# A decoder layer in one kernel: the softmax shifts of a cross-attention set through one transpose, an addition on VectorE, and another order of the first loads

## The chip, the cores and the metric

The kernel runs on one core of a Trainium2 chip. A core has five engines with a queue of instructions each: TensorE (PE in the profile; its loads of weights are listed apart as PEld), VectorE (DVE), ScalarE (ACT), GpSimd (POOL) and SyncE (SP), which here issues most of the DMAs. Each engine runs its own queue in order; semaphores make one engine wait for another. TensorE writes its results into eight banks of PSUM, from which VectorE and ScalarE read them; everything else lies in SBUF, in 128 partitions.

The metric is the device time of one execution in microseconds. It is given as the median of several runs; a profile is taken from one execution more, which has a time of its own.

## The reference

One layer of a decoder for x of 4 x 512 x 512 numbers in float32: three blocks, each behind a layer norm and added to x.

```python
x = x + _L0_attn_ref(_layernorm(x), wq_comp, wq_up, wk, wv, ..., out_w1, out_w2)   # 16 heads, window of 128
x = x + _L0_xattn_ref(_layernorm(x), ctx, ctx, mask, Wq, Wk, Wv, Wo)                # cross attention
x = x + _L0_ffn_ref(_layernorm(x), w_gate, w_up, w_down)                            # ternary feed-forward
```

The change touches the second block above all. It has 4 batches, 512 queries, 1024 keys, and 16 query heads of 32 columns in 4 groups that share keys and values:

```python
Q = (query @ Wq).reshape(b, q_len, G, Hpg, dh) / math.sqrt(dh)
K = (key @ Wk).reshape(b, kv_len, G, dh)
V = (value @ Wv).reshape(b, kv_len, G, dh)
scores = jnp.einsum('bqghd,bkgd->bghqk', Q, K) + m * rel
scores = jnp.where(mask[:, None, None, None, :], scores, neg)
out = jnp.einsum('bghqk,bkgd->bqghd', jax.nn.softmax(scores, axis=-1), V)
```

The layer norm is `(x - mean) / sqrt(var + 1e-5)` over the 512 columns of a row.

## The kernel before

The program is one long list of steps; the order of TensorE's work, and in places of ScalarE's and VectorE's, is that of the code (`manual_schedule`), while the queues of the other engines are ordered by a scheduler. The stages follow one another: a prologue (0 to 60 us of the profile), 64 units of local attention (60 to 640), a transition, cross attention (712 to 1345), its end, and the feed-forward block (from about 1400).

**The prologue.** SyncE loads, in the order of the code, the first 128 rows of x (L67), then through `fold_load` (L504) the first block of out_w1 (L509, 0.25 MB), x's rows 1 to 3 of 128 (L518), the second block of out_w1, the first of out_w2 (L512, 1 MB), and then wq_comp, wk, wv, the cosines and sines and the two norm weights (L522 to L533). The norm weights are multiplied on VectorE into kw_col (L535). On TensorE two chains are interleaved by `fill` (L908 to L912): `before(0)` takes the statistics of x's rows, normalises them (h, L125), transposes them (tr_ps, L133) and makes qc_ps (L620); `fold` multiplies out_w1 by out_w2 into one weight (w1T through L133 and L134, then f_ps, L678), one step of it for each count of `fill`.

**A layer norm's scale.** `norm_of` (L100) is used for the queries of cross attention and the rows of the feed-forward block, 12 times in all: VectorE's statistics (L87, L88), an addition of epsilon on GpSimd (L106, tiles veps2 and rstd2 with one buffer each), a power of -0.5 on GpSimd (L80), then ScalarE's shift (L113, L116) and the normalised rows (L120, called from `norm_rows`).

**Cross attention.** It works in 16 sets, m = 0 to 15, each of one batch and one of the four heads of every group. A set has 512 queries in 4 tiles of 128 (qt), 4 groups (g) and two halves of the keys (h). The softmax needs the maximum of each query's row. Two sets ahead, `row_max` (L1040) computes scores without the maximum for 128 queries and 512 keys at a time (s_ps, L1045), and VectorE reduces each to one column of nms (L1049, negated). `merge` (L1074) takes the minimum over the two halves. `shift` (L1084) turns the result from columns into rows, splits each number into a rounded part (a copy in F32R) and the rest, and moves both as two more rows, R_TOP and R_TOP + 1, into the operand qss of the scores, whose multiplication then subtracts the maximum. It takes these steps: transposes into nm_ps (L1088, a PSUM bank), a copy to nmT (L1092), a scaling by `parts` (L1093), a multiply and add from nm_ps (L1096), and the moves on SyncE (L1100, which the profile lists under the helper's line L187).

The main loop runs over steps of one tile of 128 keys, 8 for each set. In each step TensorE has: three row-max products for the set that lies ahead, two multiplications of the scores (st, L1107), a fourth row-max product between them, two more scores, what is planned beside it (`extra`: shift, queries, keys, values, outputs), the second half of the scores (L1118), and the weighted values (o_ps, L1143) of the step before. ScalarE takes two exponentials of 128 x 1024 for each step (L1125); GpSimd adds them to the sums of the softmax (L1132, 2.38 us each), and later multiplies by the reciprocal. `merge(m)` comes at the end of step 8m - 3, `shift(m)` is planned at step 8m - 2, and the scores of set m begin at step 8m.

The tiles nm_ps, s_ps, and other short products share the three PSUM banks of the pool `smp` (tag "sm"); st has two buffers of two banks, o_ps one bank.

From step 87 on, `side_rows` normalises and quantises pairs of rows of 128 for the feed-forward block, beside the attention: eight pieces each, for pairs beginning at steps 87, 93, 102, 108, 114 and 120.

Of the kernel before, what the change touches and what calls it, by code (L numbers as in the profile page):

```python
# [12 lines left out]
F32 = mybir.dt.float32  # L13
F32R = mybir.dt.float32r
# [4 lines left out]
ALU = mybir.AluOpType  # L19
AX = mybir.AxisListType  # L20
PSUM = bass.MemoryType.PSUM

P = 128
B, T, D = 4, 512, 512
# [3 lines left out]
G = 4  # L28
# [22 lines left out]
def decoder_layer(  # L51
# [48 lines left out]
    def norm_of(t0, n):  # L100

        mv = row_stats(t0, n)
        veps, rstd, shift = (
            small.tile([P, QT], F32, name=name, bufs=1) for name in ("veps2", "rstd2", "shift")
        )
        nc.gpsimd.tensor_tensor(veps[:, :n], mv[:, :n, 1], least[:, 0, :n], ALU.add)  # L106
        power_neg_half(rstd[:, :n], veps[:, :n])
        return mv, rstd, shift, n

# [75 lines left out]
    def move(out, in_, by=None):  # L185

        (by or nc.sync).dma_start(out=out.bitcast(F32), in_=in_.bitcast(F32))  # L187
# [305 lines left out]
    with tc.tile_pool(name="aw", bufs=1) as aw, tc.tile_pool(name="akv", bufs=2) as akv, \  # L493
# [10 lines left out]
        def fold_load(n, second=True):  # L504

            g, h = divmod(n, HG)
            if n not in w1s:
                w1s[n] = ap.tile([P, D], F32, name="w1")
                nc.sync.dma_start(out=w1s[n], in_=out_w1[g, ts(h, P)])  # L509
            if h == 0 and second:  # L510
                w2s[g] = ap.tile([P, DC, D], F32, name="w2")
                nc.sync.dma_start(  # L512
                    out=w2s[g], in_=out_w2[g * D:(g + 1) * D].rearrange("(c p) o -> p c o", p=P)
                )

        fold_load(0, False)
        for t in range(1, QT):
            nc.sync.dma_start(out=xres[:, t, :], in_=x[0, ts(t, P)])  # L518
        for n in (1, 0):
            fold_load(n)  # L520
        wqc_sb = aw.tile([P, DC, P], F32, name="wqc_sb")
        nc.sync.dma_start(out=wqc_sb, in_=wq_comp.rearrange("(c p) n -> p c n", p=P))  # L522
        wkv_sb = aw.tile([P, DC, 2 * P], F32, name="wkv_sb")
# [381 lines left out]
        with tc.manual_schedule(  # L905
            engines={mybir.EngineType.PE, mybir.EngineType.Activation, mybir.EngineType.DVE}
        ):
            for i, _ in enumerate(before(0)):  # L908
                if i in (0, QT - 1):
                    fill(5 if i else 1)  # L910
                elif i >= QT:
                    fill(6 if i == 9 else 2)  # L912
        with tc.manual_schedule(engines={mybir.EngineType.PE, mybir.EngineType.Activation}):
# [98 lines left out]
    with tc.tile_pool(name="b1", bufs=1) as b1, \  # L1012
# [27 lines left out]
        def row_max(m, i):  # L1040

            b, hh = divmod(m, HG)
            hf, g, qt = i // 16, i // 4 % 4, i % 4
            s_ps = smp.tile([P, T], F32, tag="sm", name="s_ps")
            nc.tensor.matmul(  # L1045
                s_ps, lhsT=qss[hh][0:R_TOP, g, ts(qt, P)], rhs=kss[b % 2][0:R_TOP, g, ts(hf, T)],
                start=True, stop=True,
            )
            nc.vector.tensor_reduce(nms[m][:, qt, g, hf:hf + 1], s_ps, AX.X, ALU.max, negate=True)  # L1049

        def row_maxima(m, i):

            b, hh = divmod(m, HG)
            hf, g, qt = i // 8, i // 4 % 2 * 2, i % 4
            s_ps = stp.tile([P, 2, T], F32, name="st")
            for j in range(2):
                nc.tensor.matmul(
                    s_ps[:, j, :], lhsT=qss[hh][0:R_TOP, g + j, ts(qt, P)],
                    rhs=kss[b % 2][0:R_TOP, g + j, ts(hf, T)], start=True, stop=True,
                )  # L1060
            nc.vector.tensor_reduce(
                nms[m][:, qt, g:g + 2, hf], s_ps, AX.X, ALU.max, negate=True
            )

        parts = small.tile([2 * G, 2], F32, name="parts", bufs=1)
        nc.vector.tensor_reduce(
            parts[:, 0:1], ident[:2 * G, 0:2 * G].rearrange("p (g h) -> p g h", h=2)[:, :, 1],
            AX.X, ALU.add,  # L1070
        )
        nc.vector.tensor_scalar(parts[:, 1:2], parts[:, 0:1], -2.0, 1.0, ALU.mult, ALU.add)

        def merge(m):  # L1074

            full = small.tile([P, QT, G, 2], F32, tag="nm3", name="nm3", bufs=2)
            both = nms[m].rearrange("p q g h -> p (q g) h").unsqueeze(2)
            nc.vector.tensor_reduce(
                full.rearrange("p q g h -> p (q g) h"), both.to_broadcast([P, QT * G, 2, 2]),
                AX.X, ALU.min,  # L1080
            )
            nms[m] = full

        def shift(m):  # L1084

            ps = smp.tile([2 * G, T], F32, tag="sm", name="nm_ps")
            for qt in range(QT):
                nc.tensor.transpose(  # L1088
                    ps[:, ts(qt, P)], nms[m][:, qt].rearrange("p g h -> p (g h)"), ident
                )  # L1090
            nmT = bx.tile([2 * G, T], F32R, tag="t", name="nmT", bufs=3)
            nc.scalar.copy(nmT, ps)  # L1092
            nc.scalar.activation(  # L1093
                nmT.bitcast(F32), nmT.bitcast(F32), AF.Copy, scale=parts[:, 1:2]
            )
            nc.vector.scalar_tensor_tensor(  # L1096
                nmT, ps, parts[:, 0:1], nmT.bitcast(F32), ALU.mult, ALU.add
            )
            for g in range(G):
                move(qss[m % HG][R_TOP:R_TOP + 2, g, :], nmT[2 * g:2 * g + 2, :])  # L1100

        def scores(m, kt, i):
            b, hh = divmod(m, HG)
# [123 lines left out]

        def side_queries(m, half):
            if half == 0:
                nms[m] = small.tile([P, QT, G, 2], F32, tag="nm2", name="nm2", bufs=2)  # L1230
            queries(m, half)
            if half == 1:
                send_queries(m)
# [45 lines left out]


        with tc.manual_schedule(engines={mybir.EngineType.PE}):
            nms[0] = small.tile([P, QT, G, 2], F32, tag="nm2", name="nm2", bufs=2)
            first.values(0)
            first.turn(2, nc.scalar)
            first.keys(2)
            first.values(1)
            first.turn(3)
            first.keys(3)
            first.send(1)
            for i in range(G * QT):  # L1290
                row_maxima(0, i)
                if i in (2, 4):
                    side_queries(1, i // 4)
                if i in (6, 8):
                    first.values(i // 2 - 1)
                if i == 8:
                    batches[1] = KeysValues(1)
                    batches[1].rows()
            merge(0)
            last = None  # L1300
            for step in range(-2, KT * SETS):
                m, kt = divmod(step, KT)
                now = 0 <= step < KT * SETS
                ahead, i0 = divmod(step + 10, KT)
                maxima = [
                    lambda i=i: row_max(ahead, 4 * i0 + i) for i in range(4)
                ] if 0 <= ahead < SETS else []
                for f in maxima[:3]:
                    f()
                sts = [scores(m, kt, 0)] if now else None  # L1310
                for f in maxima[3:]:
                    f()
                if now:
                    sts.append(scores(m, kt, 1))
                for f in extra.pop(step, []):
                    f()
                if maxima and i0 == KT - 1:
                    merge(ahead)
                ps = weights(m, kt, sts) if now else None
                if last is not None:  # L1320
                    weigh(*divmod(step - 1, KT), last)
                if kt == 1 and 1 <= m < SETS:
                    divide(m - 1, before_last)
                    spread(m - 1)
                if kt == 2 and 1 <= m < SETS:
                    reciprocals(m - 1)
                if kt == 4 and 1 <= m < SETS:
                    quotients(m - 1)
                for f in at_end.pop(step, []):
                    f()  # L1330
                before_last, last = last, ps
            ternary_load("d")
            weigh(SETS - 1, KT - 1, last)
            divide(SETS - 1, last)
            scores_pool.close()
            gup = ctx.enter_context(tc.tile_pool(name="cgu", bufs=4, space=PSUM, side="right"))
            tiles = [Tile(t) for t in range(NT)]
            tiles[0].gated_mm(0)
            tiles[0].gated_mm(1)
            for qt in range(QT):  # L1340
                quotient(SETS - 1, qt)
            for n in range(2):
                tiles[0].gated_mul(n)
                tiles[0].gated_mm(n + 2)
                output(SETS - 2, (2 * n, 2 * n + 1), 2)
            for n in range(2, 4):
                tiles[0].gated_mul(n)
            for half in range(2):
                tiles[0].first(half)
# [122 lines left out]
```

## Time and profile before

| what | us |
|---|---|
| runs: lowest, median, highest of 3 | 1684.10, 1684.86, 1688.29 |
| the profiled execution | 1683.08 |
| its span, first to last instruction | 1681.3 |
| mean granted TensorE clock over the span | 0.990 of full |

The profile is that of one execution. By stage, in us of busy time (the columns of the windows' view, rounded here):

| stage | length | PE | DVE | ACT | POOL |
|---|---|---|---|---|---|
| prologue, 0 to 60 | 60 | 47.5 | 29.8 | 12.5 | 13.3 |
| local attention, 60 to 640 | 580 | 578.6 | 448.8 | 316.9 | 160.4 |
| transition, 640 to 712 | 72 | 62.7 | 32.1 | 9.2 | 16.5 |
| cross attention, 712 to 1345 | 633 | 613.5 | 390.4 | 335.0 | 507.2 |
| its end, 1345 to 1400 | 55 | 50.1 | 30.8 | 30.2 | 14.5 |
| feed-forward, 1400 to 1681.3 | 281.3 | 266.9 | 252.6 | 222.2 | 5.2 |

The operations that the change touches, with their shapes and lengths, from the view of tiles (nanoseconds: shortest, median, longest):

```profile
L1088 PE MATMUL nm_ps<-ident,nm x64: 270/272/421, 711.8 to 1343.5; 128*8 128x128 f32 x64
L1092 ACT CAST nmT<-nm_ps x16: 558/575/577, 712.9 to 1343.8; 8x512 fp32r<-8x512 f32 x16
L1093 ACT ACTIVATE nmT<-nmT,parts x16: 702/706/721, 713.5 to 1345.2; 8x512 f32<-8x512 f32 x16
L1096 DVE SCALAR_TENSOR_TENSOR nmT<-nm_ps,parts,nmT x16: 729/730/740, 714.5 to 1346.0; 8x512 fp32r<-8x512 f32 x16
L187 SPq DMA_DIRECT2D qs<-nmT x64: 562/568/662, 715.2 to 1348.6; - x64
L106 POOL TENSOR_TENSOR veps<-mv,least x12: 195/202/1097, 262.7 to 1510.0; 128x2 f32<-128x2 f32 x8, 128x4 f32<-128x4 f32 x4
```

In such lines "L1088" is the line of the kernel, "128*8" a matmul's stationary tile, and "x64" how often it ran. A matmul's length in the records runs on while the next one has begun, so four transposes of 0.27 us each take 0.53 us together. In a timeline, the bracket at a line's end gives the engine's idle time before it and whose result ended it. The same rows with their neighbours are read below.

### The profile page before, as it was taken

To read this page: it belongs to the slowest core of one execution; us is meant where nothing else is said; L and a number is where in the kernel's file an instruction comes from. 1 tells how busy PE (TensorE), PEld (TensorE's weight loads), DVE (VectorE), ACT (ScalarE), POOL (GpSimd) and SP (SyncE) were. 2 spreads that over 40 slices of the span, in tenths; PEclk is the share of its full clock that TensorE was granted. 3 is DMA by queue.
4 is the path that set the end of the run, shared out by engine and by line. 5 is a ranking of instruction groups with operands and counts; after the bars stand their busy time and mean duration, and the time that the engine had idled before them with its cause. 6 is when DMAs were issued, how large, how long until landed. Compare 5 with 4: busy or idle time off the path is not lost.

```text
span 1681.3 us, 23544 instructions
## 1 busy us (share of the span) xinstructions
PE 1619.2 (96%) x8128; PEld 954.4 (57%) x8128; DVE 1184.4 (70%) x2357; ACT 925.9 (55%) x1871; POOL 717.0 (43%) x480
## 2 busy tenths in 40 slices
PE   7999999999999999799999999999989998999997
PEld 4566666666665666555555555555544435666664
DVE  4566887987778762665656565666657657999997
ACT  1454454555446563145444554445556765888886
POOL 2212232322223221368878787878769930000000
PEclk9999999999999999799999999999989999999999
DMA  8531312232223101421212121211112110000000
GB/s 264 146 116 51 100 51 70 77 92 82 69 77 90 54 1 33 112 52 39 58 27 72 39 58 27 69 43 39 34 66 59 37 58 3 13 14 13 20 13 32
DMA packets 96551, 99.60 MB, mean 59 GB/s; under 512 B 50884, under 2 KB 57672, under 8 KB 96008
## 3 DMA queue, kind: packets, MB, share of 16 engines
q1 hardware_dynamic: 88128, 83.51, 17.6%
q10 hardware_dynamic: 7152, 13.44, 2.5%
q0 software_dynamic: 1152, 1.15, 0.3%
q8 instruction: 64, 1.05, 0.3%
q14 instruction: 55, 0.45, 0.1%
HBM read 61.76 MB, written 10.86 MB: 43 GB/s over the span
## 4 chain that ended last, share of the span: by engine, by line
PE 80%; DVE 9%; ACT 5%; issue 2%; DMA 1%; SPq 1%; POOL 1%; ACTq 0%; DVEq 0%; POOLq 0%
PE y L690 12%; PE s_ps L1045 8%; PE st L1107 7%; PE o_ps L1143 6%; PE sc L816 5%; PE f_ps L678 3%; PE st L1118 3%; PE q_ps L295 3%; PE xo_ps L1202 3%; PE q_ps L797 3%; PE av L876 3%; PE d_ps L477 2%; PE y_ps L429 2%; PE g_ps L393 2%; PE u_ps L393 2%
## 5 line engine op out<-in xcount | busy, mean ns | idle before, releaser
L1132 POOL TENSOR_TENSOR sum<-sum,p 128x1024 f32<-128x1024 f32 x180 | 422.9, 2381 | 36.3 <-ACT p L1125 36.2
L1049 DVE TENSOR_REDUCE nm<-s_ps 128x1 f32<-128x512 f32 x480 | 300.0, 681 | 158.9 <-PE s_ps L1045 158.6
L1125 ACT ACTIVATE p<-st 128x1024 f32<-128x1024 f32 x256 | 249.4, 1020 | 95.8 <-PE st L1118 89.5
L690 PE MATMUL y<-wf,attnT 128*128 128x512 f32 x512 | 251.7, 602 | 0.0
L845 POOL TENSOR_TENSOR p<-p,den 128x512 f32<-128x512 f32 x64 | 67.0, 1047 | 356.8 <-DVE den L844 203.1
L1045 PE MATMUL s_ps<-ks,qs 99*128 99x512 f32 x480 | 183.8, 453 | 17.1 <-DVE nm L1049 10.4
L1045 PEld LDWEIGHTS s_ps<-ks,qs 99*128 99x128 f32 x480 | 82.0, 190 | 159.7 <-DVE nm L1049 50.8
L1107 PE MATMUL st<-qs,ks 101*128 101x512 f32 x512 | 164.7, 403 | 6.3 <-ACT p L1125 5.8
L1143 PE MATMUL o_ps<-p,va 128*32 128x512 f32 x1024 | 137.8, 608 | 0.0
L838 ACT ACTIVATE p<-s,nm,rs 128x128 f32<-128x128 f32 x256 | 123.2, 484 | 8.0 <-DVE nm L828 6.2
L690 PEld LDWEIGHTS y<-wf,attnT 128*128 128x128 f32 x512 | 88.0, 190 | 61.6 <-issue 59.1
L1132 POOL TENSOR_TENSOR sum<-p,p 128x1024 f32<-128x1024 f32 x30 | 70.6, 2373 | 108.8 <-ACT p L1125 95.8
L1107 PEld LDWEIGHTS st<-qs,ks 101*128 101x128 f32 x512 | 95.5, 190 | 35.6 <-ACT p L1125 20.3
L816 PE MATMUL sc<-kT,qT 128*128 128x256 f32 (+1 forms) x512 | 107.6, 353 | 0.0
L816 PEld LDWEIGHTS sc<-kT,qT 128*128 128x128 f32 x512 | 88.6, 190 | 25.8 <-issue 15.8
L80 POOL TENSOR_TENSOR rs<-ss,neghalf 128x4 f32<-128x4 f32 (+1 forms) x72 | 81.6, 1134 | 47.2 <-DVE ss L590 43.9
L809 ACT COPY qT<-qtr 128x512 f32<-128x512 f32 x64 | 37.5, 586 | 113.3 <-PE qtr L807 113.3
L890 ACT COPY attnT<-av 128x256 f32<-128x256 f32 x128 | 42.8, 375 | 82.0 <-PE av L882 74.7
L393 PEld LDWEIGHTS <-xqT 128*128 128x128 bf16 x512 | 50.0, 98 | 47.9 <-issue 1.4
L429 PE MATMUL y_ps<-had,mT 128*128 128x128 f32 x512 | 68.2, 281 | 0.0
L299 ACT ACTIVATE qH<-q_ps 128x256 fp32r<-128x256 f32 x32 | 12.3, 385 | 99.5 <-PE q_ps L295 95.3
L797 PE MATMUL q_ps<-wqu_sb,qcT 128*128 128x512 f32 x128 | 66.4, 600 | 0.0
(203 smaller groups left out, 3066.9 us busy)
## 6 DMA issues: line engine op xcount, KB each, us to landing
qs<-qH SPq DMA_DIRECT2D x128, 64.0 KB
cx<-in_ctx SPq DMA_DIRECT2D x30, 256.0 KB
w<-in_L_attn_out_w SPq DMA_DIRECT2D x16, 256.0 KB
w<-in_L_attn_out_w SPq DMA_DIRECT2D x4, 1024.0 KB
raw<-in_L_ffn_w_gate SPq DMA_DIRECT2D x4, 1024.0 KB
raw<-in_L_ffn_w_up SPq DMA_DIRECT2D x4, 1024.0 KB
raw<-in_L_ffn_w_down SPq DMA_DIRECT2D x4, 1024.0 KB
raw<-in_L_ffn_w_gate ACTq DMA_DIRECT2D x8, 512.0 KB
```

Of the source, the lines that this page charges most:

```text
L393: nc.tensor.matmul(acc, lhsT=xqTs[self.t][:, c, :], rhs=w[c][:, ts(n, 512)], start=(c == 0), stop=(c == DC - 1),)
L429: nc.tensor.matmul(y_ps[:, k, :], lhsT=self.mT[q][:, k, :], rhs=had, start=True, stop=True)
L690: nc.tensor.matmul(y, lhsT=attnT[:, h, :], rhs=wf[:, h, :], start=(h == 0), stop=(h == HEADS - 1))
L797: nc.tensor.matmul(q_ps, lhsT=made[self.b][0][:, ts(self.qt, P)], rhs=wqu_sb[:, ts(self.g, HG * P)], start=True, stop=True,)
L816: nc.tensor.matmul(sc[:, h, first * P:], lhsT=self.qT[:, h, :], rhs=kT[:, (qt - 1 + first) * P:(qt + 1) * P], start=True, stop=True,)
L838: nc.scalar.activation(self.p[:, h, :], s[:, h, :], AF.Exp, bias=nm[:, h:h + 1], scale=self.rs[:, h:h + 1], accum_out=den[:, h:h + 1],)
L1045: nc.tensor.matmul(s_ps, lhsT=qss[hh][0:R_TOP, g, ts(qt, P)], rhs=kss[b % 2][0:R_TOP, g, ts(hf, T)], start=True, stop=True,)
L1049: nc.vector.tensor_reduce(nms[m][:, qt, g, hf:hf + 1], s_ps, AX.X, ALU.max, negate=True)
L1107: nc.tensor.matmul(st[:, g % 2, :], lhsT=ks[0:R_TOP + 2, g, ts(kt, P)], rhs=qss[hh][0:R_TOP + 2, g, :], start=True, stop=False,)
L1125: nc.scalar.activation(p, st, AF.Exp)
L1132: by.tensor_tensor(sums[m][i], last[i] if kt == 1 else sums[m][i], ps[i], ALU.add)
L1143: nc.tensor.matmul(accs[m][at, :], lhsT=va[:, kt, at], rhs=ps[g // 2][:, g % 2, :], start=(kt == 0), stop=(kt == KT - 1),)
```

## The change

Three parts.

1. `norm_of`: the addition of epsilon is a `tensor_scalar` on VectorE instead of a `tensor_tensor` on GpSimd. The power stays on GpSimd.
2. The prologue: SyncE's loads come as x's first rows, first out_w1, first out_w2, second out_w1, x's rows 1 to 3, then the rest as before. TensorE's order follows: after the first transposes of h come six steps of `fold` at once (the transposes of the first and second w1 and the four multiplications of f_ps), then the other transposes of h.
3. The shifts: nms has the layout (g, qt, h) instead of (qt, g, h). `merge` writes the minima twice, as the two parts, with two reductions of 16 columns instead of one of 32 whose input is read twice. `shift` transposes all 32 columns (part, g, qt) at once into a tile of 32 partitions x 128 instead of four transposes into 8 x 512; copy, scaling and multiply-add work on 32 x 128. `parts`, the factors of each partition, changes with the layout. Two moves, one for each part, from 16 partitions of 512 B into one partition of qss, replace four moves from two partitions of 2 KB into two.

```diff
--- before.py
+++ after.py
@@ -103,7 +103,7 @@
         veps, rstd, shift = (
             small.tile([P, QT], F32, name=name, bufs=1) for name in ("veps2", "rstd2", "shift")
         )
-        nc.gpsimd.tensor_tensor(veps[:, :n], mv[:, :n, 1], least[:, 0, :n], ALU.add)
+        nc.vector.tensor_scalar(veps[:, :n], mv[:, :n, 1], LN_EPS, None, ALU.add)
         power_neg_half(rstd[:, :n], veps[:, :n])
         return mv, rstd, shift, n
 
@@ -513,11 +513,10 @@
                     out=w2s[g], in_=out_w2[g * D:(g + 1) * D].rearrange("(c p) o -> p c o", p=P)
                 )
 
-        fold_load(0, False)
+        for n in range(2):
+            fold_load(n)
         for t in range(1, QT):
             nc.sync.dma_start(out=xres[:, t, :], in_=x[0, ts(t, P)])
-        for n in (1, 0):
-            fold_load(n)
         wqc_sb = aw.tile([P, DC, P], F32, name="wqc_sb")
         nc.sync.dma_start(out=wqc_sb, in_=wq_comp.rearrange("(c p) n -> p c n", p=P))
         wkv_sb = aw.tile([P, DC, 2 * P], F32, name="wkv_sb")
@@ -906,8 +905,8 @@
             engines={mybir.EngineType.PE, mybir.EngineType.Activation, mybir.EngineType.DVE}
         ):
             for i, _ in enumerate(before(0)):
-                if i in (0, QT - 1):
-                    fill(5 if i else 1)
+                if i == 0:
+                    fill(6)
                 elif i >= QT:
                     fill(6 if i == 9 else 2)
         with tc.manual_schedule(engines={mybir.EngineType.PE, mybir.EngineType.Activation}):
@@ -1046,7 +1045,7 @@
                 s_ps, lhsT=qss[hh][0:R_TOP, g, ts(qt, P)], rhs=kss[b % 2][0:R_TOP, g, ts(hf, T)],
                 start=True, stop=True,
             )
-            nc.vector.tensor_reduce(nms[m][:, qt, g, hf:hf + 1], s_ps, AX.X, ALU.max, negate=True)
+            nc.vector.tensor_reduce(nms[m][:, g, qt, hf:hf + 1], s_ps, AX.X, ALU.max, negate=True)
 
         def row_maxima(m, i):
 
@@ -1059,36 +1058,30 @@
                     rhs=kss[b % 2][0:R_TOP, g + j, ts(hf, T)], start=True, stop=True,
                 )
             nc.vector.tensor_reduce(
-                nms[m][:, qt, g:g + 2, hf], s_ps, AX.X, ALU.max, negate=True
-            )
-
-
-
-        parts = small.tile([2 * G, 2], F32, name="parts", bufs=1)
+                nms[m][:, g:g + 2, qt, hf], s_ps, AX.X, ALU.max, negate=True
+            )
+
+
+
+        parts = small.tile([2 * G * QT, 2], F32, name="parts", bufs=1)
         nc.vector.tensor_reduce(
-            parts[:, 0:1], ident[:2 * G, 0:2 * G].rearrange("p (g h) -> p g h", h=2)[:, :, 1],
-            AX.X, ALU.add,
+            parts[:, 0:1],
+            ident[:2 * G * QT, G * QT:2 * G * QT], AX.X, ALU.add,
         )
         nc.vector.tensor_scalar(parts[:, 1:2], parts[:, 0:1], -2.0, 1.0, ALU.mult, ALU.add)
 
         def merge(m):
 
-            full = small.tile([P, QT, G, 2], F32, tag="nm3", name="nm3", bufs=2)
-            both = nms[m].rearrange("p q g h -> p (q g) h").unsqueeze(2)
-            nc.vector.tensor_reduce(
-                full.rearrange("p q g h -> p (q g) h"), both.to_broadcast([P, QT * G, 2, 2]),
-                AX.X, ALU.min,
-            )
+            full = small.tile([P, 2, G, QT], F32, tag="nm3", name="nm3", bufs=2)
+            for part in range(2):
+                nc.vector.tensor_reduce(full[:, part], nms[m], AX.X, ALU.min)
             nms[m] = full
 
         def shift(m):
 
-            ps = smp.tile([2 * G, T], F32, tag="sm", name="nm_ps")
-            for qt in range(QT):
-                nc.tensor.transpose(
-                    ps[:, ts(qt, P)], nms[m][:, qt].rearrange("p g h -> p (g h)"), ident
-                )
-            nmT = bx.tile([2 * G, T], F32R, tag="t", name="nmT", bufs=3)
+            ps = smp.tile([2 * G * QT, P], F32, tag="sm", name="nm_ps")
+            nc.tensor.transpose(ps, nms[m].rearrange("p h g q -> p (h g q)"), ident)
+            nmT = bx.tile([2 * G * QT, P], F32R, tag="t", name="nmT", bufs=3)
             nc.scalar.copy(nmT, ps)
             nc.scalar.activation(
                 nmT.bitcast(F32), nmT.bitcast(F32), AF.Copy, scale=parts[:, 1:2]
@@ -1096,8 +1089,12 @@
             nc.vector.scalar_tensor_tensor(
                 nmT, ps, parts[:, 0:1], nmT.bitcast(F32), ALU.mult, ALU.add
             )
-            for g in range(G):
-                move(qss[m % HG][R_TOP:R_TOP + 2, g, :], nmT[2 * g:2 * g + 2, :])
+            for part in range(2):
+                row = qss[m % HG][R_TOP + part:R_TOP + part + 1]
+                move(
+                    row.rearrange("o g (q j) -> o (g q) j", j=P),
+                    nmT[part * G * QT:(part + 1) * G * QT, :],
+                )
 
         def scores(m, kt, i):
             b, hh = divmod(m, HG)
@@ -1227,7 +1224,7 @@
 
         def side_queries(m, half):
             if half == 0:
-                nms[m] = small.tile([P, QT, G, 2], F32, tag="nm2", name="nm2", bufs=2)
+                nms[m] = small.tile([P, G, QT, 2], F32, tag="nm2", name="nm2", bufs=2)
             queries(m, half)
             if half == 1:
                 send_queries(m)
@@ -1279,7 +1276,7 @@
 
 
         with tc.manual_schedule(engines={mybir.EngineType.PE}):
-            nms[0] = small.tile([P, QT, G, 2], F32, tag="nm2", name="nm2", bufs=2)
+            nms[0] = small.tile([P, G, QT, 2], F32, tag="nm2", name="nm2", bufs=2)
             first.values(0)
             first.turn(2, nc.scalar)
             first.keys(2)
```

## The prediction

> **What bounds the kernel now.** The page's table of busy time comes first, then its chain, then busy time by stage. The chain of waits is made of TensorE:
>
> ```profile
> PE 1619.2 (96%) x8128; PEld 954.4 (57%) x8128; DVE 1184.4 (70%) x2357; ACT 925.9 (55%) x1871; POOL 717.0 (43%) x480
> ...
> PE 80%; DVE 9%; ACT 5%; issue 2%; DMA 1%; SPq 1%; POOL 1%; ACTq 0%; DVEq 0%; POOLq 0%
> ```
>
> The view of windows (PE, PEld, DVE, ACT and POOL busy us, clock, DMA) tells where PE leaves anything:
>
> ```profile
> 60.00:640.00 580.00, 578.59 (x2356) 357.27 (x2355) 448.79 (x1183) 316.86 (x1011) 160.36 (x165) 1.00 0.25 72
> ...
> 712.00:1345.00 633.00, 613.46 (x3332) 332.53 (x3330) 390.39 (x672) 334.99 (x469) 507.15 (x240) 0.99 0.18 48
> ```
>
> Local attention idles for 1.4 us, so what the prologue gains or loses in front of it reaches the end. Cross attention idles for 19.5 us, and a matmul that waits inside its queue is counted busy. So I read the place of the change itself, in the timeline (start, length, engine, work, idle before and its releaser), for set 1:
>
> ```profile
> 747.18 0.60 PE L1088 MATMUL nm_ps<-ident,nm 128*8 128x128 f32 x4
> 747.71 0.51 PE L1118 MATMUL st<-qL,kL 32*128 32x512 f32 x4
> 747.82 0.57 ACT L1092 CAST nmT<-nm_ps 8x512 fp32r<-8x512 f32 x1 [1.62 <-PE nm_ps L1088]
> 748.32 1.02 ACT L1125 ACTIVATE p<-st 128x1024 f32<-128x1024 f32 x1
> 749.15 0.73 PE L1045 MATMUL s_ps<-ks,qs 99*128 99x512 f32 x2
> 749.24 0.71 ACT L1093 ACTIVATE nmT<-nmT,parts 8x512 f32<-8x512 f32 x1
> 749.69 0.69 DVE L1049 TENSOR_REDUCE nm<-s_ps 128x1 f32<-128x512 f32 x1 [1.58 <-PE s_ps L1045]
> 750.29 0.73 DVE L1096 SCALAR_TENSOR_TENSOR nmT<-nm_ps,parts,nmT 8x512 fp32r<-8x512 f32 x1
> 750.43 0.50 PE L1045 MATMUL s_ps<-ks,qs 99*128 99x512 f32 x1 [0.55 <-DVE nm L1049]
> 750.77 0.63 PE L1107 MATMUL st<-qs,ks 101*128 101x512 f32 x2
> 751.24 0.40 PE L1045 MATMUL s_ps<-ks,qs 99*128 99x512 f32 x1
> ```
>
> The tile of the shift (nm_ps) holds one of three PSUM banks from 747.18 until the DVE step L1096 ends at 751.0. The row-max products (s_ps) have only two banks meanwhile, so the third waits for the first one's reduction. An ordinary step runs them without a wait; st follows s_ps after 0.81 us there, after 1.62 here:
>
> ```profile
> 753.47 0.98 PE L1045 MATMUL s_ps<-ks,qs 99*128 99x512 f32 x3
> 754.28 0.62 PE L1107 MATMUL st<-qs,ks 101*128 101x512 f32 x2
> ```
>
> **The change: shift and merge, 16 times.** Four transposes, 0.53 us of PE (747.18 to 747.71), become one; a transpose in the groups of four takes 0.11 to 0.13, but alone it also fills and drains, so I take 0.20: 0.33 saved. The copy reads 128 columns in place of 512: 0.575 by L1092 before, 0.27 by L581 (a 128x128 copy). The scaling: 0.706 before, about 0.38 by L299 (128x256, 0.385). L1096: 0.730 before, 0.26 estimated below L300's 0.425 for 256 columns. The merge's two reductions of 16 columns cost about 0.15 each (L1068, 0.14; L348, 0.15) against one of 0.216: 0.1 more on DVE, which waits 158.9 us for s_ps in this stage. SP issues two moves (568 ns each) in place of four, 1.1 us less; they have two steps, over 7 us, until set m's scores read them, so rows of 512 B cost nothing unless they land 5 us later. In the order of instructions ACT now scales ahead of its two exponentials, not between them, so nmT is done some 1.3 us after the transpose in place of 3.8, and all three banks are back when the third s_ps wants one. Set 1 then gains 0.33 + (1.62 - 0.81) = 1.14 us. Site by site:
> - Sets 1, 3, 4, 7, 8, 11 look like this: 6 x -1.14 = -6.8.
> - Sets 5 and 9 have two statistics of 0.68 beside it on DVE: 2 x -0.9 = -1.8.
> - Set 0 runs cold, each step on the chain: transposes 0.89 to 0.25, copy -0.30, scaling -0.32, L1096 -0.47, together -1.7; taken as -1.5.
> - Set 15, partly behind other waits: -0.6.
>
> **The addition of the row scale (L106), 12 times,** leaves POOL (0.202 us) for DVE (0.155 by L96). At sets 2, 6, 10 this makes a wait: veps2 has one buffer, so the addition waits until POOL's pow has read the one before (791.53 to 792.56 at set 2, behind two sums of 2.38), and on DVE it now stands ahead of L1096 and the reductions. L1096 then starts at about 792.7, as before (792.63), the first reduction about 1 us later than now (791.54), and PE waits for these: the 1.14 is lost and 0.2 more: 3 x +0.2 = +0.6. Without that wait it would be -0.5 each. In the feed-forward stage POOL is idle (5.24 us busy), so 0.
>
> The last quarter has the pairs of feed-forward rows, whose pow (POOL) ACT waits for. At set 12 the wait of ACT (5.44) and PE (4.12) stays, as pow is behind the same four sums; after it copy, scaling and L1096 are 1.1 us shorter and one exponential is out of the way: -1.9, but at 1241 ACT has L113 and L116 ahead of the exponentials (+0.4) and is itself the limit, so between -1.5 and 0: -0.7. At set 13 the order moves pow behind two more sums:
>
> ```profile
> 1278.10 0.70 POOL L80 TENSOR_TENSOR rstd<-veps,neghalf 128x2 f32<-128x2 f32 x1
> 1278.77 4.74 POOL L1132 TENSOR_TENSOR sum<-sum,p 128x1024 f32<-128x1024 f32 x2
> ...
> 1278.83 0.48 ACT L113 ACTIVATE shift<-mv,rstd 128x1 f32<-128x1 f32 x2
> ```
>
> Those sums then end at about 1282.6, pow at 1283.3, L113 and L116 (0.48 + 0.20) at 1284.0; the exponentials queued behind them start there, not at 1280.52, and the st that waits for their bank starts at 1285.0, not 1282.21: +2.8, the site's own gain included. The clock may fall: the 4.12 us of idle at 1222 are followed by 4 us at 0.50 and 4 at 0.85 (2.6 us lost), the 2.37 before 1241.23 by 0.80 and 0.77 over 8 (1.7 lost). I add 1.2, between 0 and 2.6: +4.0. Set 14, with L113 moved ahead of two exponentials: +0.7.
>
> Sum: -6.8 - 1.8 - 1.5 - 0.6 + 0.6 - 0.7 + 4.0 + 0.7 = -6.1 us.
>
> [...] First the rows: the two DVE additions at 1369.58 that run beside POOL's quotient (1.38) took 1.1 us more than their like, 2.31 against 1.22; but small one-tensor steps beside POOL's sums (L348 0.153, L351 0.163) are not stretched, and the addition is nearer to these. [...]
>
> **The prologue's loads.** PE and DVE before:
>
> ```profile
> 11.05 1.12 PE L133 MATMUL tr_ps<-ident,h 128*128 128x128 f32 x4 [3.25 <-DVE h L125]
> ...
> 16.22 1.09 PE L133 MATMUL tr_ps<-ident,h 128*128 128x128 f32 x4 [2.53 <-DVE h L125]
> ...
> 17.96 4.85 PE L678 MATMUL f_ps<-w,w1T 128*128 128x512 f32 x8
> 22.64 1.88 PE L620 MATMUL qc_ps<-hT,wqc_sb 128*128 128x512 f32 x4
> ```
>
> ```profile
> 15.42 0.16 DVE L535 SCALAR_TENSOR_TENSOR kw_col<-kq_col 128x1 f32<-128x1 f32 x1 [2.96 <-DMA kq_col<-in_L_attn_q_norm_w]
> ```
>
> After the change the first f_ps (4.85) stands ahead of three of the four transposes of h. Its w2 (1 MB) comes second on SP's queue; with what is ahead of it that is 1.5 MB at 161 to 277 GB/s (0 to 8 us), so 7 to 8 us, and f_ps runs in about 9 to 14. The rows x1 to x3 land 1.25 MB later, 4 us at 277 to 351 GB/s, but h2 and h3 waited until 15.5 for kw_col anyway, whose load has the same bytes ahead of it. DVE now has h2 behind kw_col too: h2 at 16.0, h3 at 16.7, its transposes to 18.2, the copy 0.59, qc at 18.9 against 22.64: -3.7. PE idles at 14 to 16, so qc may run at half clock: 0 to 2 back. Taken: -3.0; bounds -4 and +2 (loads late by more than the slack).
>
> Total -9.1 us. The profiled execution took 1683.08 (span 1681.3 and 1.8 around it), 1.8 below the median shown, 1684.86; 9.1 off that is 1675.8.
>
> **The rivals.** What this kernel's measurement can tell from no change is 0.3%, 5 us: faster is below 1679.8, slower above 1689.9.
> - *The bank was not the limit.* If exponentials or reductions hold PE as long as before, a site gives only its transposes: 16 x -0.33 = -5.3; with +4.0 and +0.7 and the prologue, -3.6: 1681, no change. For it: ACT's exponentials L1125 follow st, and no wait over 0.55 us is shown at set 1. Against: the ordinary step is 0.81 shorter.
> - *The loads give nothing*, as kw_col, DMA or the cold clock decide: -6.1, 1679. For it: 1.07 and 1.12 of DMA share at 8 to 16 us.
> - *Pow behind the sums* (slower). If ACT or DVE queue behind pow at three places of the last quarter, not one, each costs what set 12's shows, 4.1 of wait and 2.6 to 3.4 of clock, about 7. That is 2 x 7 more: +5, 1690; with the loads giving nothing as well, 1693. It decides once two more of the six pairs have pow moved behind two sums. For it: POOL is busy for 507 of 633 us. Against: the order shows only one moved so.
> - *The change does not do what it says:* 48 fewer PE instructions stand in the order, so it does.
>
> **The numbers.** The forecast has 0.60 (its own range 1668 to 1682), no bank limit 0.15, loads giving nothing 0.12, pow 0.13. Faster: 0.52 of the forecast, 0.08 of the loads, 0.02 of the bank: 0.62. Slower: 0.11 of pow, 0.02 of the rest: 0.13. No change: 0.25. The range 1666 to 1688 leaves out most of pow (0.11) and 0.07 below.
>
> **What would show it.** Right: nm_ps followed by s_ps x3 in one row with st 0.8 behind; qc near 19; one PE wait of about 3 us near 1280. Wrong: a wait of DVE for POOL at many additions, or st still 1.6 behind s_ps; then the 1.14 was not the bank's.

## The result

The changed kernel is slower: 1703.91 us median (1701.96 to 1707.55) beside 1685.96 for the kernel before (1684.10 to 1688.29), ratio 1.0115 with a 95% interval of 1.0102 to 1.0127. Its profiled execution took 1701.96 us, with a span of 1700.1, 18.8 more than before's.

The page of the kernel after, its table of busy time, its chain and its wait line for the row-max products:

```profile
PE 1626.4 (96%) x8048; PEld 957.0 (56%) x8080; DVE 1192.2 (70%) x2385; ACT 917.3 (54%) x1871; POOL 712.5 (42%) x468
...
PE 77%; DVE 9%; ACT 6%; issue 4%; DMA 2%; POOL 2%; SPq 1%; ACTq 0%; DVEq 0%; POOLq 0%
...
L1044 PE MATMUL s_ps<-ks,qs 99*128 99x512 f32 x480 | 184.3, 457 | 24.9 <-DVE nmT L1089 13.4
```

The wait line on the page of the kernel before (the numbers behind the bars are busy us, mean ns of one, idle us before it and what ended most of that idle time):

```profile
L1045 PE MATMUL s_ps<-ks,qs 99*128 99x512 f32 x480 | 183.8, 453 | 17.1 <-DVE nm L1049 10.4
```

No total stands out: VectorE is busy 7.8 us longer, GpSimd 4.5 shorter, TensorE 7.2 longer. PE's share of the chain fell from 80% to 77%, and PE's idle time before s_ps rose from 17.1 to 24.9 us. Before, the ordinary reductions (L1049) ended most of it; now the shift's last step does (L1089, which was L1096). Shares do not say where that happens. The starts of each set's shift do (nm_ps in the timelines, us):

| start of | before | after | difference |
|---|---|---|---|
| qc_ps (prologue) | 22.64 | 18.51 | -4.13 |
| exponentials of local attention | 61.09 | 60.73 | -0.37 |
| shift of set 1 | 747.18 | 748.17 | +0.99 |
| set 2 | 789.05 | 789.88 | +0.83 |
| set 3 | 831.13 | 835.98 | +4.84 |
| set 6 | 961.35 | 963.14 | +1.79 |
| set 7 | 1003.46 | 1012.88 | +9.42 |
| set 10 | 1133.52 | 1140.04 | +6.53 |
| set 11 | 1175.61 | 1187.04 | +11.43 |
| set 13 | 1269.70 | 1281.13 | +11.43 |
| set 14 | 1307.70 | 1324.53 | +16.82 |
| set 15 | 1343.16 | 1360.25 | +17.09 |
| end of the span | 1681.27 | 1700.11 | +18.85 |

Between sets 3 and 6 and between 7 and 10 the changed kernel gains about 1 us for each set. It loses 4.0, 7.6 and 4.9 us behind the shifts of sets 2, 6 and 10, together 16.5, and 5.4 behind that of set 13. The timeline of the changed kernel at set 6 (start, length, engine, work; in brackets idle time and who ended it) shows what happens there; the lines of GpSimd, VectorE and TensorE are put one after the other (line numbers moved with the edit: the sums are L1129 now, L1132 before):

```profile
965.65 1.03 POOL L80 TENSOR_TENSOR rstd<-veps,neghalf 128x4 f32<-128x4 f32 x1
966.67 4.62 POOL L1129 TENSOR_TENSOR sum<-sum,p 128x1024 f32<-128x1024 f32 x2
...
966.71 4.61 DVE L106 TENSOR_SCALAR veps<-mv 128x2 f32<-128x2 f32 x1 [3.07 <-POOL rstd L80]
971.24 0.33 DVE L1089 SCALAR_TENSOR_TENSOR nmT<-nm_ps,parts,nmT 32x128 fp32r<-32x128 f32 x1
...
971.62 0.80 PE L1044 MATMUL s_ps<-ks,qs 99*128 99x512 f32 x1 [6.11 <-DVE nmT L1089]
```

At the same place of the kernel before, VectorE waited 0.40 us ahead of the shift's last step, and TensorE 0.55 us for a bank; the addition was GpSimd's:

```profile
964.60 0.50 PE L1045 MATMUL s_ps<-ks,qs 99*128 99x512 f32 x1 [0.55 <-DVE nm L1049]
964.94 0.74 DVE L1096 SCALAR_TENSOR_TENSOR nmT<-nm_ps,parts,nmT 8x512 fp32r<-8x512 f32 x1 [0.40 <-POOL rstd L80]
964.95 0.20 POOL L106 TENSOR_TENSOR veps<-mv,least 128x2 f32<-128x2 f32 x1
```

In the changed kernel VectorE first waits 3.07 us for GpSimd's power, then takes 4.61 us over an addition of 128 x 2 numbers. It begins within 0.04 us of GpSimd's next two sums and ends 0.03 us after them. The shift's last step stands behind it, PE waits 6.11 us for the bank, and then runs at half clock (0.50 from 970 to 975). All twelve additions, in the view of line 106 (shortest, median, longest, ns):

```profile
L106 DVE TENSOR_SCALAR veps<-mv x12: 146/170/4607, 262.3 to 1526.3; 128x2 f32<-128x2 f32 x8, 128x4 f32<-128x4 f32 x4
```

Four of them are long: 2.31 (set 2), 4.61 (set 6), 2.32 (set 10) and 3.44 us (set 13); the other eight take 0.15 to 0.17.

The shift itself does what the prediction said of it. Set 1 in the changed kernel:

```profile
748.17 0.28 PE L1083 MATMUL nm_ps<-ident,nm 128*32 128x128 f32 x1
748.38 0.51 PE L1115 MATMUL st<-qL,kL 32*128 32x512 f32 x4
...
749.81 0.96 PE L1044 MATMUL s_ps<-ks,qs 99*128 99x512 f32 x3
750.61 0.63 PE L1104 MATMUL st<-qs,ks 101*128 101x512 f32 x2
```

TensorE starts the next product 0.21 us behind the one transpose, 0.53 us behind the first of the four before. The three row-max products are in one row, as in an ordinary step, and st follows 0.80 us behind them, 1.62 before.

### The profile page after: what moved, and what is told of

Read it like the earlier page. It is cut to its first block, busy times and chain, and to the rows that moved or that the text cites. A ratio compares the mean times of both kernels' runs of the same rounds, so it can differ in the third digit from the quotient of the medians.

```text
span 1700.1 us, 23369 instructions
## 1 busy us (share of the span) xinstructions
PE 1626.4 (96%) x8048; PEld 957.0 (56%) x8080; DVE 1192.2 (70%) x2385; ACT 917.3 (54%) x1871; POOL 712.5 (42%) x468
## 3 DMA queue, kind: packets, MB, share of 16 engines
q8 instruction: 64, 1.05, 0.3%
## 4 chain that ended last, share of the span: by engine, by line
PE 77%; DVE 9%; ACT 6%; issue 4%; DMA 2%; POOL 2%; SPq 1%; ACTq 0%; DVEq 0%; POOLq 0%
PE y L689 12%; PE s_ps L1044 7%; PE st L1104 6%; PE o_ps L1140 5%; PE sc L815 5%; PE q_ps L295 3%; PE xo_ps L1199 3%; PE st L1115 3%; PE q_ps L796 3%; PE av L875 3%; PE f_ps L677 3%; PE d_ps L477 2%; PE y_ps L429 2%; ACT p L1122 2%; PE u_ps L393 2%
## 5 line engine op out<-in xcount | busy, mean ns | idle before, releaser
L1129 POOL TENSOR_TENSOR sum<-sum,p 128x1024 f32<-128x1024 f32 x180 | 422.5, 2377 | 44.1 <-ACT p L1122 43.5
L1044 PE MATMUL s_ps<-ks,qs 99*128 99x512 f32 x480 | 184.3, 457 | 24.9 <-DVE nmT L1089 13.4
L1104 PE MATMUL st<-qs,ks 101*128 101x512 f32 x512 | 168.2, 410 | 7.8 <-ACT p L1122 6.3
L1129 POOL TENSOR_TENSOR sum<-p,p 128x1024 f32<-128x1024 f32 x30 | 70.5, 2372 | 120.3 <-ACT p L1122 103.7
L80 POOL TENSOR_TENSOR rstd<-veps,neghalf 128x2 f32<-128x2 f32 (+2 forms) x19 | 17.2, 905 | 159.9 <-DVE veps L106 136.6
L1115 PE MATMUL st<-qL,kL 32*128 32x512 f32 x512 | 66.5, 509 | 0.0
```

The source lines that it names most:

```text
L80: nc.gpsimd.tensor_tensor(dst, src, neghalf[:, :src.shape[1]], ALU.pow)
L1044: nc.tensor.matmul(s_ps, lhsT=qss[hh][0:R_TOP, g, ts(qt, P)], rhs=kss[b % 2][0:R_TOP, g, ts(hf, T)], start=True, stop=True,)
L1104: nc.tensor.matmul(st[:, g % 2, :], lhsT=ks[0:R_TOP + 2, g, ts(kt, P)], rhs=qss[hh][0:R_TOP + 2, g, :], start=True, stop=False,)
L1115: nc.tensor.matmul(sts[g // 2][:, g % 2, :], lhsT=kL[at, ts(kt, P)], rhs=qLs[m][at, :], start=False, stop=True,)
L1129: by.tensor_tensor(sums[m][i], last[i] if kt == 1 else sums[m][i], ps[i], ALU.add)
```

## The experiments

### The addition back on GpSimd, and the addition alone

The first kernel is the changed one without its first part; the second is the kernel before with that part alone.

```diff
-        nc.vector.tensor_scalar(veps[:, :n], mv[:, :n, 1], LN_EPS, None, ALU.add)
+        nc.gpsimd.tensor_tensor(veps[:, :n], mv[:, :n, 1], least[:, 0, :n], ALU.add)
```

> The changed kernel with the addition of epsilon (L106) back on GpSimd; loads and shifts stay changed. Theory P (VectorE's addition waits for GpSimd: first for the power that still reads the one buffer, 3.1 us at sets 2, 6 and 10, then for the sums that run beside it, 2.31 to 4.61 us in place of 0.15): the 4.0, 7.6 and 4.9 us that the changed kernel loses after these three sites go, and each site gains 0 to 1.0 like the others; 1703.9 - 16.5 - 1.5, about 1686, between 1683 and 1689. Rival S (the shortened shift itself, with both exponentials behind it, makes PE wait at these sites): stays above 1700.

Measured: 1679.42 us, ratio to before 0.9967 (0.9954 to 0.9980), 24.5 us less than the changed kernel's median. The shifts of sets 3, 7 and 11 start 1.51, 5.39 and 9.05 us earlier than before, with no loss at 2, 6 or 10. It is faster than theory P expected (1683 to 1689). Beside the profile of the changed kernel, whose span is 24.1 us longer, the three sites account for 19.0: they stop losing and gain 0.8 each. Of the rest 1.6 lie ahead of the first shift, 0.9 at set 12 and 2.8 behind set 15's shift, where no experiment was made.

> The kernel before with the addition on VectorE and nothing else. Theory P: sets 2, 6 and 10 lose here as well, 4 to 8 us each with the half clock behind the wait; 1686 + 12 to 20, that is 1698 to 1706. Rival S: the addition costs 12 x 0.15 at most, 1685 to 1688. The prologue and the other sites are to stay within 0.3 us of before under both.

Measured: 1704.14 us, ratio 1.0116 (1.0097 to 1.0135). Up to set 2 it runs within 0.25 us of before; then it loses 5.7 us at set 2, 5.5 at set 6 and 5.3 at set 10. Rival S falls: three additions in the wrong place make 16.4 of the 18.4 us that the span grows by, with the old shift as with the new. Another 1.4 us come behind set 13, where one more addition is held for 2.29 us.

### The wait or the hold

Two things happen to the addition: it waits for the power, since veps2 has one buffer, and then it is held beside the sums. The next kernel changes only the kind of instruction: a reduction over one element, which copies the variance and leaves epsilon out. All orders and waits are those of the changed kernel.

```diff
-        nc.vector.tensor_scalar(veps[:, :n], mv[:, :n, 1], LN_EPS, None, ALU.add)
+        nc.vector.tensor_reduce(veps[:, :n], mv[:, :n, 1:2], AX.X, ALU.max)
```

Theory K, in this run and the next, is that the kind of instruction decides whether it is held.

> The changed kernel with VectorE's tensor_scalar at L106 replaced by a tensor_reduce of one element with the same input and output (a copy; epsilon is left out of the sum). Every engine's order and every wait stay the same; only the kind of instruction differs. [...] Rival W (the wait for the power is what costs, or any VectorE instruction on this tile is held): L106 stays at 2 to 4.6 us and the time at 1702 to 1706; or, if L106 is short and the time above 1698, the wait alone costs it.

Measured: 1685.65 us, ratio 1.0008 (0.9998 to 1.0017). Line 106, and VectorE and GpSimd at set 6:

```profile
L106 DVE TENSOR_REDUCE veps<-mv x12: 128/155/157, 261.6 to 1511.9; 128x2 f32<-128x2 f32 x8, 128x4 f32<-128x4 f32 x4
```

```profile
963.59 0.15 DVE L106 TENSOR_REDUCE veps<-mv 128x2 f32<-128x2 f32 x1 [3.06 <-POOL rstd L80]
963.81 0.34 DVE L1089 SCALAR_TENSOR_TENSOR nmT<-nm_ps,parts,nmT 32x128 fp32r<-32x128 f32 x1
...
963.55 7.06 POOL L1129 TENSOR_TENSOR sum<-sum,p 128x1024 f32<-128x1024 f32 x3
```

The wait is the same, 3.06 us; the hold is gone, with the same sums beside it. Sets 2, 6 and 10 now cost 2.0, 0.45 and 1.7 us. So of the 16.5 us about 4.1 belong to the wait and 12.4 to the hold and the half clock behind it. (Beside the kernel with the addition on GpSimd, where these sites gain 2.4, the addition costs 19.0: 6.6 by the wait and 12.4 by the hold.) So the kind of instruction decides, as theory K has it: in the same place the addition took 4.61 us and the reduction 0.15. Neither of rival W's two cases came: line 106 is short, and the time is below 1698.

```diff
-            small.tile([P, QT], F32, name=name, bufs=1) for name in ("veps2", "rstd2", "shift")
+            small.tile([P, QT], F32, name=name, bufs=4 if name == "veps" else 1) for name in ("veps", "rstd2", "shift")
```

> The changed kernel with the sum of variance and epsilon in a tile of four buffers instead of one, so that VectorE's addition no longer waits for the power on GpSimd; it stays a tensor_scalar. Theory K: L106 is still held beside GpSimd's sums, up to 2.4 us or two sums (4.6) in several of nine places, and the scheduler puts it ahead of other work: 1692 to 1704. Rival W: without the wait the cost goes: 1684 to 1689, and L106 at 0.15.

Measured: 1680.97 us, ratio 0.9979 (0.9969 to 0.9989): faster than before, outside what theory K expected and below rival W's range. The hold is there, as K says (line 106 takes 2.39 us twice and 3.43 once), but it costs nothing: the sets with the two 2.39 gain 0.9 each, as in the other kernels. VectorE and TensorE of this kernel beside set 5:

```profile
928.33 2.39 DVE L106 TENSOR_SCALAR veps<-mv 128x2 f32<-128x2 f32 x1
930.64 0.68 DVE L1048 TENSOR_REDUCE nm<-s_ps 128x1 f32<-128x512 f32 x1
...
931.22 0.95 PE L1044 MATMUL s_ps<-ks,qs 99*128 99x512 f32 x3
```

Without the wait the scheduler puts the addition elsewhere, behind most of the step's reductions while TensorE has a long product of values; TensorE's next row-max products start without a wait. So the loss takes both in one place: the wait without the hold cost 4.1 us, and the hold without the wait, at other places, nothing. The single buffer pinned the addition in front of the shift's last step, and the hold made it long there. A hold at that place without the wait was not run.

### Which instructions are held

```diff
-        nc.vector.tensor_scalar(veps[:, :n], mv[:, :n, 1], LN_EPS, None, ALU.add)
+        nc.vector.tensor_tensor(veps[:, :n], mv[:, :n, 1], least[:, 0, :n], ALU.add)
```

> The changed kernel with VectorE's addition as a tensor_tensor of two SBUF inputs (the variance and a tile of epsilons) in place of a tensor_scalar; orders and waits stay the same. [...]

Measured: 1698.41 us, ratio 1.0072 (1.0057 to 1.0087). The addition with two inputs is held as well: line 106 takes 4.61, 4.60 and 2.30 us at sets 2, 6 and 10. VectorE and GpSimd at set 6:

```profile
970.18 4.60 DVE L106 TENSOR_TENSOR veps<-mv,least 128x2 f32<-128x2 f32 x1 [3.07 <-POOL rstd L80]
...
970.13 4.62 POOL L1129 TENSOR_TENSOR sum<-sum,p 128x1024 f32<-128x1024 f32 x2
```

At set 6 an addition with one SBUF tensor took 4.61 us and one with two 4.60; the reduction took 0.15. The long ones stand beside the sums of 128 x 1024. In local attention an addition of the changed kernel runs inside a GpSimd power of 128 x 4 numbers and takes 0.15 us (with two inputs 0.14, beside the same power):

```profile
406.55 1.01 POOL L80 TENSOR_TENSOR rs<-ss,neghalf 128x4 f32<-128x4 f32 x1 [2.03 <-DVE ss L589]
407.00 0.15 DVE L106 TENSOR_SCALAR veps<-mv 128x4 f32<-128x4 f32 x1
```

### The other two parts by themselves

The kernel before with only the second part of the change's list (loads), and with only the third (shift and merge); the diffs are those parts of the change.

> The kernel before with the shift and merge of the change alone (loads in the old order, addition on GpSimd). Theory P: the shift is the whole gain and GpSimd's late power the loss behind it: -0.8 to -1.1 us at each of twelve sites, about -9.5 at set 12's shift, then +5.4 between the shifts of sets 13 and 14 as with the loads changed; -4.5 in all, 1677 to 1682. Rival L (the loads bring part of the 4.6 us that the kernel with the addition on GpSimd gained): 1681 to 1685.

Measured: 1679.80 us, ratio 0.9961 (0.9948 to 0.9974). The shift of set 12 starts 7.3 us earlier than before, 9.1 counted from the shift of set 0; 5.8 are lost again between sets 13 and 14. ScalarE, GpSimd and TensorE there:

```profile
1276.48 0.48 ACT L113 ACTIVATE shift<-mv,rstd 128x1 f32<-128x1 f32 x2 [3.98 <-POOL rstd L80]
...
1273.43 2.36 POOL L1130 TENSOR_TENSOR sum<-sum,p 128x1024 f32<-128x1024 f32 x1
1275.74 0.71 POOL L80 TENSOR_TENSOR rstd<-veps,neghalf 128x2 f32<-128x2 f32 x1
...
1278.16 1.11 PE L1105 MATMUL st<-qs,ks 101*128 101x512 f32 x2 [3.71 <-ACT p L1123]
```

This is the late power of the prediction: it is the shift's reordering that moves it behind two more sums, not the move of the addition.

> The kernel before with the prologue's loads and TensorE's order there alone. Theory P: qc_ps starts 3 us earlier, gives 1 to 1.5 back to the half clock and 1 to 2 to VectorE's statistics behind later x rows; local attention starts 1.1 us earlier to 1.8 later, and the time is that of before within 2 us: 1682 to 1686. Rival L: 3 us or more faster, 1679 to 1681.

Measured: 1682.33 us beside 1686.26, ratio 0.9984 (0.9973 to 0.9995): a small gain, 2.7 us by the ratio, between 0.8 and 4.6. In its profile qc_ps starts at 18.69 and local attention 2.31 us earlier, but at the shift of set 0 only 0.17 of that are left, and the span is 1.3 us longer than before's: from 680 to 692 us the mean granted clock is 0.57, before 0.75. So the profile does not show where the gain lies. With the shifts beside them the loads show no further gain (0.9967 with, 0.9961 without). One profile each cannot weigh so little: kernels with the old loads start local attention at 61.09 (before), 62.14 (shifts alone) and 60.87 us (addition alone).

### The rows moved

The shifts alone, with the first two pairs of feed-forward rows begun one step later and one earlier.

```diff
-        for pair, step in enumerate((87, 93, 102, 108, 114, 120)):
+        for pair, step in enumerate((88, 92, 102, 108, 114, 120)):
```

> The shifts alone, and the first pair of feed-forward rows planned one step later (88 for 87), the second one step earlier (92 for 93). In the order of instructions the power at set 13 then stands behind 180 sums as before the change (182 with it), and ScalarE's L113 at set 12 behind 196 exponentials in place of 192, with 168 sums ahead of its power as before. Theory Q (the late losses are ScalarE's queue behind a power that waits for GpSimd's backlog): the +5.4 us at set 13 goes, and at set 12 most of PE's 4.12 and 2.37 us of waiting with 2 to 4 us of half clock: 1667 to 1675. Rival R (GpSimd's backlog holds exponentials or sums in any order): 1677 to 1682 as with the shifts alone.

Measured: 1668.62 us, ratio 0.9896 (0.9879 to 0.9912), the fastest here. GpSimd and ScalarE at set 13:

```profile
1264.72 0.70 POOL L80 TENSOR_TENSOR rstd<-veps,neghalf 128x2 f32<-128x2 f32 x1
1265.40 2.38 POOL L1130 TENSOR_TENSOR sum<-sum,p 128x1024 f32<-128x1024 f32 x1
...
1265.46 0.48 ACT L113 ACTIVATE shift<-mv,rstd 128x1 f32<-128x1 f32 x2 [0.94 <-POOL rstd L80]
```

ScalarE waits 0.94 us there, not 3.98, and the shift of set 14 starts 0.9 us earlier against before than set 13's, where the shifts alone lost 5.8. At set 12 TensorE still waits 2.81 us for the shift, but the second wait behind it is gone: 4.6 us gained. Theory Q holds for set 13 and in part for set 12.

> The changed kernel with the addition on GpSimd and the two pairs of rows moved (88 and 92): the shifts, the loads and the moved rows together. If the loads are worth by themselves what they gave alone (ratio 0.9984, 2 to 4 us), 1664.5 to 1667; if local attention's start and the clock at the first shift take it back, as with the shifts (1679.4 with the loads, 1679.8 without), 1667.5 to 1669.5.

Measured: 1670.54 us, ratio 0.9917 (0.9900 to 0.9933); the intervals with and without the loads overlap, so beside the other parts the loads add nothing that this can tell. The time is above both ranges that were expected.

## Why the prediction was wrong

The forecast was 1676 us, faster; the step that failed is the addition's price. The prediction named both halves of the mechanism, the wait and the hold, and gave the one too small a number and counted the other as nothing. Of the 27.9 us between the forecast and the measured span (-9.1 and +18.8) the addition makes 15.9.

- **The addition, "+0.2" for each of sets 2, 6, 10.** Measured 4.0, 7.6 and 4.9: 16.5 us in place of 0.6. The wait for the power in front of L1096 was foreseen and is worth 4.1 by the reduction's run, not 0.6. The hold is worth 12.4. It was weighed and set aside: the prediction took 0.155 us "nearer to" L348 and L351, small one-tensor steps that are not stretched beside the sums (0.153 and 0.163). L348 is a reduction, L351 a reciprocal; the size was alike, the kind was not. The row that told it was the additions at 1369.58, 1.1 us longer beside GpSimd's product (L1190, which the prediction calls a quotient). In the runs additions with one input and with two are both held beside the sums, for 2.3 to 4.6 us each; 4.6 is more than one whole sum (2.38). Holds through two sums, the half clock behind them (0.50 from 970 to 975 at set 6) and the larger wait were in no term of the forecast.
- **Shift and merge.** Sets 1, 3, 4, 7, 8, 11: -5.5 measured between their shifts and the next (-6.8 predicted), sets 5 and 9 -1.7 (-1.8), set 15 -0.75 (-0.6). Five of the six are between -1.01 and -1.17; set 1 is at -0.16: its first scores wait 0.96 us for the two moves. The shift's last step ended at 749.55, but SP issued the moves at 752.84, behind its moves of keys. "They have two steps, over 7 us" left SP's queue out:

```profile
750.31 2.44 SPq L187 DMA_DIRECT2D ks<-kL  x4
752.84 1.17 SPq L187 DMA_DIRECT2D qs<-nmT  x2
...
755.36 0.70 PE L1104 MATMUL st<-qs,ks 101*128 101x512 f32 x2 [0.96 <-DMA qs<-nmT]
```

- **Set 0, -1.5 predicted:** +0.9 between its shift and that of set 1. The shift is shorter, but the half clock lasts longer: the product of keys behind it takes 3.62 us in place of 1.96. The other profiles show that this does not go with the new shift. From 714 to 718 us the mean granted clock is 1.00 before and 0.50 here; with the loads alone, and so the old shift, it is 0.52 and the set loses 1.3; with the new shift and the moved rows it is 0.83 and the set gains 1.0. Why the clock comes back sooner or later stays open.
- **Set 13, +4.0 predicted:** +5.4, the same without the addition's move (5.4) and with the shifts alone (5.8); the mechanism is the predicted one. Set 14: +0.7 predicted, +0.3. Set 12: -0.7 predicted, +1.05 in this profile, +0.1 with the addition on GpSimd.
- **The prologue, -3.0:** qc_ps starts at 18.51 (18.9 predicted), but local attention only 0.37 us earlier, and set 0's shift not at all (+0.05). The first half of qc_ps runs cold, 3.68 us at a mean granted clock of 0.54 for 1.88 at 1.00, inside the 0 to 2 that were allowed; then at 43 to 45 TensorE waits 0.76 for VectorE and 0.85 for GpSimd. By the view of waits VectorE had lost 6.0 us to later rows of x, whose issues the prediction did not follow; that this made the two waits is read from the order and was not tried. By itself the part gave 2.7 by the ratio, near the size predicted, but its profile lost its lead behind local attention, so it is not shown that what the prologue gains reaches the end.
- **The rival that ended slower** (power behind sums at three places) named the right engine and the wrong mechanism: the power is late at one new place only, as the prediction's main line had it, and the loss is VectorE's.
- **The last tiles,** 0 predicted, +2.5: their final products fell into half clock (5.27 us at a mean granted clock of 0.64 for 3.63 at 1.00) in this profile. I read this as the clock's timing; no run was made for it, and the profile of the changed kernel with the addition on GpSimd does not have it.

## What to carry to other kernels

Before a small VectorE step is priced by a row beside GpSimd's work, take a row of the same kind of instruction: beside the sums (2.3 to 2.4 us each) additions of SBUF tensors took 2.3 to 4.6 us, small reductions 0.15 to 0.16. Then ask what stands behind it in the queue: wait and hold cost 4 to 8 us in front of a PSUM release and the hold cost nothing in a step with slack. Where a helper engine runs a backlog, the planned step of the work that waits for it is a cheap lever: two numbers in a plan gave 11 us here beside the new shifts, more than the change set out to gain. With the old shifts they were not tried.

## What the runs showed that was not expected

The hold can last longer than one GpSimd instruction: three additions of 0.15 us (two of them with two inputs) took 4.6, through two sums of 2.3 each with no gap between them, while others beside such pairs got through after one (2.31). Two numbers per partition were enough: the additions of 128 x 2 at sets 6, 10 and 13 took 4.61, 2.32 and 3.44 us. And the clock: TensorE's wait of 2.81 us at set 12 of the kernel with the moved rows is followed by a mean granted clock of 0.64 over four microseconds:

```profile
1215.95 0.49 PE L1045 MATMUL s_ps<-ks,qs 99*128 99x512 f32 x1 [2.81 <-DVE nmT L1090]
...
1216.00:1220.00 4.00, 3.96 (x8) 2.12 (x9) 2.54 (x5) 3.29 (x8) 3.49 (x2) 0.64 0.11 25
```
